# A graph-attention layer and a ternary FFN on one core: the first layernorm spread over three engines, ten inspection pieces moved to the output projection, k2 three pairs ahead

## The chip, the cores and the metric

One NeuronCore of a Trainium2 chip runs the whole program. The time is the device time of one execution in microseconds (us); of several executions the median is given. The profile comes from one further execution, taken by the hardware profiler.

## The reference

All tensors are float32. x has 384 rows (nodes) of 1024. There are 12288 edges with a source, a destination and a type.

```python
def layernorm(x): return (x - mean(x)) / sqrt(var(x) + 1e-5)          # along the row

def gnn(x):                                          # 16 heads of 64
    q, k, v = x @ wq.T + bq, x @ wk.T + bk, x @ wv.T + bv             # 1024 -> 1024 each
    q2, k2, v2 = q @ wiq.T + biq, k @ wik.T + bik, v @ wiv.T + biv    # again, then split into heads
    w = softplus(edge_type_weights)
    mask = full((384, 384), -inf); mask[src, dst] = w[type - 1]       # the last edge of a cell wins
    diagonal: where it is -inf, w[3]
    scores = q2 @ k2.T / 8 + mask                    # per head
    return (softmax(scores) @ v2) @ wo.T + bo

def ffn(x):                                          # weights in {-1, 0, 1}
    h = silu((x @ w1.T) * w1_s) * ((x @ w2.T) * w2_s)                 # 1024 -> 512
    h = gelu((h @ h1.T) * h1_s)                                       # 512 -> 512
    h = gelu((h @ h2.T) * h2_s)                                       # 512 -> 512
    return (h @ w3.T) * w3_s                                          # 512 -> 1024

x = x + gnn(layernorm(x))
x = x + ffn(layernorm(x))
```

## The kernel before

The 384 rows are three row tiles of 128 (`NT`), the 1024 features eight blocks of 128 (`KF`). A projection that keeps its result transposed (`matmul_T`, line 141: features on the partitions, 384 rows along the free dimension) adds eight products per output block; one that keeps rows on the partitions (`matmul_R`, line 150) adds eight products of 512 columns. A float32 product is two TensorE instructions in the profile.

Tile, the layer in which the kernel is written, sets all semaphores. Line 57 fixes the order on SyncE, ScalarE, VectorE and TensorE to that of the source: each of these engines runs its instructions in the order in which they are written, and one that waits holds up all behind it on its engine. This holds for the DMAs that SyncE and ScalarE issue too. POOL's order is Tile's own. A buffer of a pool comes free for the next tile with its tag when the last reader of the old one is done.

**Front.** ScalarE's queue loads the four edge type weights (`wt`), the edges (`ed`, three rows per partition) and the per-feature vectors (`vec`); SyncE's queue loads the three tiles of x (line 65) and the first half of wq. POOL makes the identity, a diagonal mask and two small tables (lines 189 to 197). VectorE computes the start of softplus, two constants (`later`, `bare`) and the edge keys source*384 + destination (lines 201 to 213), and then, tile by tile, statistics, mean and deviation, scales and the left half of the normalised row (`layernorm`, line 120); ScalarE computes the square root and the right half. `transpose_in` (line 132) turns each tile on TensorE, and ScalarE copies it into `xT`.

**Mask.** The keys are written to memory and read back as rows, eight columns at a time (`keys`, line 247). `targets` (line 256) sends an edge that is followed by another of the same cell to a spare cell. `scatter` (line 276) writes 128 edge values at once into a table in memory by an indirect DMA from POOL; each of the 96 waits for the one two before it. At the end the table is read back as `nmask` (line 300), which attention adds to its scores. Line 291 writes the table's start (`bare`), and lines 292 and 298 prefetch weights in between.

**Projections.** q, q2, v, v2 and k follow in this order, 64 products each (48 wider ones for v2). Weights come in halves of 2 MB through a pool of four buffers: after each half `prefetch` queues the next load, which waits for the oldest buffer.

**Inspection.** The FFN weights are ternary in the inputs at hand. The kernel checks this: `inspect` (line 310) loads 16 pieces of 128 x 1024 of w1, w2, h1, h2 and w3 and ORs their bits into `bits`, two VectorE instructions a piece. Four pieces follow q in the source, six follow q2, six v2. After k the 512 columns are halved down to one, summed over the partitions on TensorE and kept as `flag` (lines 352 to 362). If no low bit is set, `rest(True)` computes the FFN with rounded weights and a two-part split of the activations; otherwise `rest(False)` computes it in full float32. Line 471, ahead of the output projection, loads the flag into a register of every engine, on which the branch of line 610 depends.

**Attention.** A unit is one pair of heads and one row tile, 24 in all. Each turn of the loop of line 449 writes the scores of unit u, the transposes of unit u-2, every third turn the weighted sum of a pair, and some of the 64 products of k2: 16 (two blocks, that is two pairs of heads) stand ahead of the loop, 48 are spread over the first 20 turns.

**Output projection.** For each row tile two halves of wo are applied (`project_out`, line 490): eight products, then VectorE adds the result to x and takes statistics. `layernorm` follows, and `transpose_x2` turns the tile for the FFN: tile 0 after tile 1 is projected, tile 1 between the halves of tile 2, tile 2 within the FFN. PSUM holds three such results (`ps_mm`).

## Time and profile before

| | us |
|---|---|
| three runs | 434.35, 2401.24, 434.09; median 434.35 |
| profiled execution | 432.71 |
| its span, first to last instruction | 430.8 |
| TensorE busy | 407.4 |
| VectorE busy | 177.4 |
| POOL busy | 111.8 |
| ScalarE busy | 100.1 |
| first product of q | 18.8 |
| first and last scatter | 25.1, 228.2 |
| mask used first | 238.9 |
| first product with wo | 330.6 |
| first product of the FFN | 373.3 |

In a line of the timeline or of a group stand the engine (PE is TensorE, PEld its weight loads, DVE VectorE, ACT ScalarE, SPq the DMAs that SyncE issues), the line of the source, the operation, output and input by their names, and in brackets how long the engine was idle before and what ended that. In the chain of waits each line is a piece of the path that ended last: start, length and what it was. The slices divide the span into 40 equal parts; a digit is the busy share in tenths.

### The profile page before, as it was taken

The page shows a single profiled execution, that of the slowest core. Times are in us where ns is not written, and L with a number is a line of the kernel's source. Part 1 is how long each engine was busy: PE and PEld are TensorE (multiplying, and loading weights), DVE is VectorE, ACT ScalarE, POOL GpSimd, SP SyncE. Part 2 cuts the span into 40 slices and gives each one's busy share as a digit, 9 for nine tenths or more (in the row PEclk, how much of TensorE's full clock was granted, in tenths as well). Part 3 has the DMA queues.
Part 4 walks back from the last instruction along what each step waited for, and adds up shares of the span by engine and source line. Part 5 has one row for each costly group of instructions (what it writes and reads, how often), then busy time and mean ns, then how long its engine had stood idle before and what let it go on. Part 6 is the DMA issues. An engine that isn't in the chain of part 4 may idle for free.

```text
span 430.8 us, 4238 instructions
## 1 busy us (share of the span) xinstructions
PE 407.4 (95%) x1515; PEld 239.7 (56%) x1515; DVE 177.4 (41%) x562; ACT 100.1 (23%) x221; POOL 111.8 (26%) x117
## 2 busy tenths in 40 slices
PE   0799999999999999999999899999999999999992
PEld 0555555555555544455555455555545444699982
DVE  2945869422240011005400476655663133423354
ACT  4511111111111000001111555445464011131420
POOL 3023335243344574754374400000000000200000
PEclk9999999999999999999999999999999999999998
DMA  7699766979764405066706104100060000750012
GB/s 253 219 359 245 257 164 161 390 265 339 273 175 168 174 21 196 0 234 205 247 0 209 41 2 136 60 1 0 2 195 2 0 0 0 212 179 2 1 50 100
DMA packets 28023, 59.64 MB, mean 138 GB/s; under 512 B 4352, under 2 KB 5216, under 8 KB 27872
## 3 DMA queue, kind: packets, MB, share of 16 engines
q1 hardware_dynamic: 20688, 50.12, 34.8%
q0 software_dynamic: 6880, 9.03, 7.4%
q8 instruction: 14, 0.23, 0.2%
q10 hardware_dynamic: 432, 0.18, 0.1%
q14 instruction: 9, 0.07, 0.0%
HBM read 57.06 MB, written 2.26 MB: 138 GB/s over the span
## 4 chain that ended last, share of the span: by engine, by line
PE 77%; DMA 11%; DVE 5%; POOL 2%; issue 2%; ACT 2%; ACTq 0%; DVEq 0%; POOLq 0%
PE ps L146 29%; PE ps L155 19%; PE ps L379 7%; PE ps L516 6%; PE sc L395 4%; PE pp L428 4%; PE av L437 4%; DMA tab<-val,cell 4%; PE ps L529 3%; POOL tab L278 2%; DMA raw<-in_h 2%; DMA ed<-in_edges 2%; DMA out<-y 2%; DMA nmask<-tab 1%; DVE st L102 1%
## 5 line engine op out<-in xcount | busy, mean ns | idle before, releaser
L278 POOL DMA_INDIRECT tab<-val,cell x96 | 96.5, 1005 | 128.6 <-DMA tab<-val,cell 75.1
L262 DVE SCALAR_TENSOR_TENSOR jk<-kr,key,later 128x256 bf16<-128x256 f32 x96 | 39.9, 479 | 14.8 <-DMA kr<-keyd 14.8
L379 PE MATMUL ps<-kT,wik 128*128 128x384 f32 x128 | 45.6, 493 | 0.0
L146 PE MATMUL ps<-xT,wq 128*128 128x384 f32 x128 | 43.0, 500 | 0.0
L317 DVE TENSOR_TENSOR bits<-bits,raw 128x512 int32<-128x512 int32 x32 | 22.1, 692 | 50.7 <-DMA raw<-in_w 39.0
L155 PE MATMUL ps<-wo,aT 128*128 128x512 f32 x96 | 41.8, 593 | 0.0
L146 PE MATMUL ps<-qT,wiq 128*128 128x384 f32 x128 | 41.4, 486 | 0.0
L146 PE MATMUL ps<-xT,wv 128*128 128x384 f32 x128 | 41.4, 486 | 0.0
L146 PE MATMUL ps<-xT,wk 128*128 128x384 f32 x128 | 41.4, 486 | 0.0
L155 PE MATMUL ps<-wiv,vT 128*128 128x512 f32 x96 | 41.4, 592 | 0.0
L409 DVE CUSTOM_DVE_ANT_0 s<-sc,nmask 128x384 f32<-128x384 f32 x48 | 24.8, 553 | 26.0 <-PE sc L395 14.2
L146 PEld LDWEIGHTS ps<-xT,wq 128*128 128x128 f32 x128 | 25.0, 196 | 17.6 <-issue 1.2
L146 PEld LDWEIGHTS ps<-xT,wk 128*128 128x128 f32 x128 | 24.3, 190 | 17.2 <-issue 0.5
L146 PEld LDWEIGHTS ps<-qT,wiq 128*128 128x128 f32 x128 | 24.3, 190 | 17.0
L146 PEld LDWEIGHTS ps<-xT,wv 128*128 128x128 f32 x128 | 24.3, 190 | 17.0
L379 PEld LDWEIGHTS ps<-kT,wik 128*128 128x128 f32 x128 | 22.6, 190 | 15.5 <-issue 4.1
L155 PEld LDWEIGHTS ps<-wiv,vT 128*128 128x128 f32 x96 | 18.2, 190 | 22.7 <-issue 22.5
L155 PEld LDWEIGHTS ps<-wo,aT 128*128 128x128 f32 x96 | 18.0, 190 | 22.1 <-issue 22.1
L412 ACT ACTIVATE e<-s,lo 128x384 f32<-128x384 f32 x48 | 29.1, 609 | 3.2 <-DVE lo L409 3.1
L516 PE MATMUL ps<-x,w 128*128 128x384 f32 (+2 forms) x176 | 25.8, 306 | 0.0
L395 PE MATMUL sc<-k2T,q2T 64*128 64x384 f32 x96 | 23.5, 535 | 2.1 <-DVE lo L409 2.1
L344 DVE TENSOR_TENSOR v<-ps,row 128x512 f32<-128x512 f32 x6 | 4.2, 692 | 51.8 <-PE ps L155 51.8
(100 smaller groups left out, 355.2 us busy)
## 6 DMA issues: line engine op xcount, KB each, us to landing
kr<-keyd SPq DMA_DIRECT2D x11, 576.0 KB, 5.8
raw<-in_w SPq DMA_DIRECT2D x12, 512.0 KB, 4.8
w<-in_w POOLq DMA_DIRECT2D x3, 2048.0 KB, 9.5
wq<-in_wq SPq DMA_DIRECT2D x2, 2048.0 KB, 11.0
wiq<-in_wiq SPq DMA_DIRECT2D x2, 2048.0 KB, 14.1
wv<-in_wv SPq DMA_DIRECT2D x2, 2048.0 KB, 16.5
wiv<-in_wiv SPq DMA_DIRECT2D x2, 2048.0 KB, 10.0
wk<-in_wk SPq DMA_DIRECT2D x2, 2048.0 KB, 8.3
```

The costliest lines, as they stand in the source:

```text
L146: nc.tensor.matmul(ps[:, :N], lhsT=w[:, k, o * P:(o + 1) * P], rhs=src[:, k, :], start=(k == 0), stop=(k == nk - 1))
L155: nc.tensor.matmul(ps[:, :w.shape[2]], lhsT=src[:, k, t * P:(t + 1) * P], rhs=w[:, k, :], start=(k == 0), stop=(k == nk - 1))
L262: nc.vector.scalar_tensor_tensor(jk[:, :w], krf[:, j * P:j * P + w], key[:, c:c + 1], later[:, :w], op0=ALU.is_equal, op1=ALU.mult, accum_ ...
L278: i = nc.gpsimd.indirect_dma_start(out=tab, in_=val[:, c:c + 1], in_offset=None, out_offset=bass.IndirectOffsetOnAxis(ap=cell[:, c:c + 1], ...
L317: nc.vector.tensor_tensor(bits, bits, raw[:, h * FH:(h + 1) * FH].bitcast(I32), op=ALU.bitwise_or)
L379: nc.tensor.matmul(ps[:, :N], lhsT=wik[o // 4][:, k, o % 4 * P:(o % 4 + 1) * P], rhs=kT[:, k, :], start=(k == 0), stop=(k == KF - 1))
L395: nc.tensor.matmul(sc[:, :N], lhsT=q2T[r, pair, t * P:(t + 1) * P], rhs=k2T[r, pair, :], start=True, stop=True)
L409: nc.vector.tensor_tensor_reduce(s, sc[:, :N], nmask[:, t, :], 1.0, 3e38, op0=ALU.add, op1=ALU.min, accum_out=lo)
L412: nc.scalar.activation(e, s, AF.Exp, bias=lo, scale=-1.0, accum_out=dens[u][:, j:j + 1])
L428: nc.tensor.transpose(pt[:, m, :], e[:, m * P:(m + 1) * P], ident)
L437: nc.tensor.matmul(av[j * D:(j + 1) * D, :N], lhsT=v2[:, m, h * D:(h + 1) * D], rhs=pTs[pair % 2][:, j * NT + m, :], start=(m == 0), stop= ...
L516: nc.tensor.matmul(ps[:, rows], lhsT=w[:, k, o * P:(o + 1) * P], rhs=x[:, k, rows], start=n == 0, stop=n == len(todo) - 1)
```

## The change

The front is written out. x comes first: the left half of tile 0 on SyncE's queue and its right half on ScalarE's, then tiles 1 and 2 on SyncE's, and the edges behind the half on ScalarE's. `vec` and `wt` are loaded between two parts of the first half of wq. `later` and `bare` are made on POOL. The steps of the three tiles are interleaved; POOL computes the left half of tiles 0 and 1, VectorE that of tile 2, and copies out of PSUM are shared by ScalarE and VectorE. TensorE transposes the identity 24 times at the start and four times after tile 0. The keys are computed before tile 2 is scaled and written after the last copy; softplus follows.

```diff
-    wt = const.tile([P, 4], FP, name="wt")
-    nc.scalar.dma_start(wt, bass.AP(tensor=etw.tensor, offset=etw.offset, ap=[[0, P], [1, 4]]))
+    xs = act.tile([P, NT, F], FP, name="xs")
+    for queue, c in ((nc.sync, slice(0, FH)), (nc.scalar, slice(FH, F))):
+        queue.dma_start(xs[:, 0, c], x[:P, c])
+    for t in (1, 2):
+        nc.sync.dma_start(xs[:, t, :], x[t * P:(t + 1) * P, :])
     ed = const.tile([P, 3, NCOL], I32, name="ed")
     nc.scalar.dma_start(ed, edges)
-    xs = act.tile([P, NT, F], FP, name="xs")
-    for t in range(NT):
-        nc.sync.dma_start(xs[:, t, :], x[t * P:(t + 1) * P, :])
-    nc.scalar.dma_start(vec, vecs)
+    def load_small():
+        nc.sync.dma_start(vec, vecs)
+        nc.sync.dma_start(wt, ...)
...
-    prefetch()
+    prefetch(load_small)                 # wq's first half in two parts, load_small between
...
+        nc.gpsimd.tensor_scalar(later, jp, 0.0, None, op0=ALU.is_gt)
+        nc.gpsimd.tensor_scalar(bare, nmask, 0.0, FAR, op0=ALU.is_equal, op1=ALU.mult)
...
+        with tc.tile_pool(name="ps_up", bufs=5, space=bass.MemoryType.PSUM) as ps_up:
+            warm(24)
+            statistics(0, sts[0], 0)
+            statistics(0, sts[0], 1)
+            deviation(0)
+            statistics(1, sts[1], 0)
+            scales(0)
+            normal(0, nc.gpsimd)
+            turned(0)
+            warm(4)
+            statistics(1, sts[1], 1)
+            deviation(1)
+            evicted(0, 0, nc.scalar.copy)
+            statistics(2, sts[2], 0)
+            scales(1)
+            normal(1, nc.gpsimd)
+            turned(1)
+            statistics(2, sts[2], 1)
+            deviation(2)
+            evicted(0, 1, nc.scalar.copy)
+            nc.vector.tensor_copy(edf, ed[:, 0:2, :])
+            nc.vector.scalar_tensor_tensor(key, edf[:, 0, :], float(N), edf[:, 1, :],
+                                           op0=ALU.mult, op1=ALU.add)
+            scales(2)
+            normal(2, nc.vector)
+            kt = ps_mm.tile([P, 512], FP, tag="mm", name="kt")
+            nc.tensor.transpose(kt[:NCOL, :P], key, ident)
+            turned(2)
+            evicted(1, 0, nc.vector.tensor_copy)
+            evicted(1, 1, nc.scalar.copy)
+            evicted(2, 0, nc.vector.tensor_copy)
+            evicted(2, 1, nc.scalar.copy)
+            nc.vector.tensor_copy(keyr, kt[:NCOL, :P])
+            nc.sync.dma_start(keyd, keyr)
```

The helpers do what their names say: `warm(n)` transposes the identity n times, `deviation` is the mean, variance and square root, `scales` the reciprocal and the scaled mean, `normal(t, engine)` the left half on that engine and the right half on ScalarE, `turned` the eight transposes, `evicted` one of the two copies out of PSUM.

The inspections after q and q2 go; the six after v2 stay. The other ten, the halving and the flag move into the output projection. Three of them at a time use a buffer of the tag "t" (that of qT, vT, kT and pTa).

```diff
         qT = project(xT, "qT", vec[:, BQ:])
-        inspect(4)
         project(qT, "q2T", biqs, dst=q2T, scale=-0.125)
-        inspect(6)
...
-    low_bits = nc.values_load(flag[0:1, 0:1], min_val=0, max_val=P * 0xFFF)
...
+    inspect_more(True, 2)                # three pieces in a buffer "t", two in "stage"
     for t in range(NT):
         st = small.tile([P, 2, 6], FP, name="st")
         project_out(t, 0, st)
-        if t == 2:
+        if t == 0:
+            inspect_more(True)
+        elif t == 1:
+            bitf = gather_bits()
+        else:
             transpose_x2(1)
         project_out(t, 1, st)
         layernorm(t, xn[:, t, :], st)
-        if t == 1:
+        if t == 0:
+            inspect_more(False, len(pieces))
+        elif t == 1:
+            fl = ps_mm.tile([P, 512], FP, tag="mm", name="fl")
+            nc.tensor.matmul(fl[:1, :1], lhsT=bitf, rhs=ones, start=True, stop=True)
+            flag = const.tile([1, 1], I32, name="flag")
+            nc.vector.tensor_copy(flag, fl[:1, :1])
+            low_bits = nc.values_load(flag[0:1, 0:1], min_val=0, max_val=P * 0xFFF)
             transpose_x2(0)
```

Ahead of attention three blocks of k2 are computed instead of two, and the loop spreads the remaining 40 products over its first 20 turns.

```diff
+AHEAD = 3
...
-        done = 0
-        for _ in range(2 * KF):
+        done, rest_k2 = 0, (KF - AHEAD) * KF
+        for _ in range(AHEAD * KF):
             next(k2)
...
-            share = min((u + 1) * 6 * KF // (units - 4), 6 * KF)
+            share = min((u + 1) * rest_k2 // (units - 4), rest_k2)
```

## The prediction

> **What bounds the kernel now.** I read the page's busy table and its slices first, then the chain of waits in order of time, then the timeline of the places that the diff touches.

> ```profile
> PE 407.4 (95%) x1515; PEld 239.7 (56%) x1515; DVE 177.4 (41%) x562; ACT 100.1 (23%) x221; POOL 111.8 (26%) x117
> PE   0799999999999999999999899999999999999992
> ```

> TensorE is busy for 407 of 430.8 us. Its work stays the same in the change, so only what it waits for can move the time: most of the 23 us it is idle lies in the first two slices and in the last, with small holes near 240 and 320 us.

> ```profile
> 1.17 7.04 DMA ed<-in_edges
> ...
> 18.92 125.42 PE ps L146 x384
> ...
> 228.18 5.53 DMA tab<-val,cell
> ...
> 234.33 4.31 DMA nmask<-tab
> ...
> 330.69 27.66 PE ps L155 x64
> ```

> This is the chain: the edge list holds up the layernorm, then TensorE runs unbroken, then the mask read back from the table opens attention (first use 238.87), then TensorE again. Between the ends stands a second chain that TensorE doesn't see until 238: 96 scatters on POOL, one after another.

> ```profile
> 8.23 0.26 DVE L210 CAST edf<-ed 128x192 f32<-128x192 int32 x1 [0.84 <-DMA ed<-in_edges]
> ...
> 18.77 11.41 PE L146 MATMUL ps<-xT,wq 128*128 128x384 f32 x30
> ...
> 20.21 0.34 PEld L146 LDWEIGHTS ps<-xT,wq 128*128 128x128 f32 x1 [0.30 <-issue]
> ...
> 20.85 0.34 PEld L146 LDWEIGHTS ps<-xT,wq 128*128 128x128 f32 x1 [0.30 <-issue]
> ...
> 91.68 0.96 POOL L278 DMA_INDIRECT tab<-val,cell  x1 [3.68 <-DMA tab<-val,cell]
> ...
> 226.90 0.97 POOL L278 DMA_INDIRECT tab<-val,cell  x1 [0.30 <-issue]
> ```

> VectorE can't start on x (landed at 0.75+5.4 = 6.2 us) before the edges are in, and the first projection starts at 18.8. Its first instructions come 0.64 us apart, later ones 125.42/384 = 0.327. Each matmul of the source is two such instructions (64 per projection, x128 in the page), so one costs 0.653 us. The scatters are 1.27 us apart where nothing else moves and wait 3 to 5 us more per pair under bulk loads.

> ```profile
> 358.19 1.04 PE L485 MATMUL pt<-ident,xn 128*128 128x128 f32 x8
> ...
> 358.39 0.69 DVE L493 TENSOR_TENSOR xs<-ps,xs 128x512 f32<-128x512 f32 x1 [5.38 <-PE ps L155]
> ...
> 360.69 0.54 DVE L123 TENSOR_SCALAR xn<-xs,mv,rs 128x512 f32<-128x512 f32 x1
> ```

> At the end of row tile 1 in the wo stage TensorE goes straight on, while VectorE still has 2.9 us of layernorm before it.

> [...] 0.64 against 0.327 us, though TensorE was 70% busy from 11.5 to 17 us; only the unbroken run from 17 released it, near 21.5. [...] scatters land 2.1 us (median) after issue in 127 to 186 us, where the DMA share is 0.33, and 5.3 in 75 to 127, where it is 0.82. [...]

> **Part 1, front.** The chain after, with rows of before. x tile 0 goes over two queues ahead of the edges' 384 small rows: I take it landed at 5.0 instead of 6.2, tile 1 at 7.5 instead of 7.9, tile 2 near 9. In VectorE's order the first half statistics of tile 1 (0.68) stand before the scales of tile 0 (0.16+0.16): so tile 0 can be normalised from 8.6. GpSimd's half isn't in the trace; [...] the tensor add of line 349 is 2.32 for 1024 with two inputs. I take 1.0 (0.8 to 1.5). The two constants moved to POOL (1152 and 256 elements, 1.5 to 3.2 us from the same rows) follow its last iota at 4.1 and end by 7.3, hidden by the wait for x. From 8.6 ScalarE is longest: three half rows (0.81), two square roots (0.30), four copies (0.59) are 5.4 us, plus 0.4 of waiting for GpSimd and the first transposes: 14.4. VectorE's last copy, which the first four products need, ends near 14.2. Projection starts at 14.3: **4.5 us** gained (3.3 to 5.5). wq's first half needs x, edges and 1 MB, 2.65 MB; before, that much had moved by 10.5 us, so it is in.

> 24 transposes of the identity at 0.24 us (1.94 for eight) run from 2.3 to about 8 without a hole, so the clock is probably up[...]. Before, the first 30 instructions took 11.41 instead of 30 x 0.327 = 9.8: **1.6 us** gained (0 to 1.6).

> **Part 2, scatter chain.** The keys now leave after the evictions: 13.9 + 3.3 landing + 3.6 for the first row block = 20.8, against 18.6. Exp and Ln with two table loads (1.28 each) go from 14.4 to 17.4 on ScalarE, before the first projection's copy; negw is there at 17.5. The second half of wq is queued on SP behind keys and `bare` as before, near 19 + 9.4, needed at 14.3 + 21 = 35. First scatter 27.2 instead of 25.06: 2.1 us later. Against that ten inspection loads (5 MB) leave the time of the scatters. From 25 to 229 the chain took 204 us where 96 x 1.27 = 122 would do: 82 us over, for 24 MB of weights (second half of wq to first half of wo), 6.8 of key rows, 8.4 of inspections and 1.6 of bias rows, 41 MB: 2.0 us per MB. Ten pieces are 5.2 MB, so 10.4 us (7 to 15). The mask then lands at 238.65 + 2.1 - 10.4 = 230.4. TensorE comes to attention at 237.4 - 6.1 + 5.2 (eight matmuls of k2 more, 8 x 0.653) = 236.5. The mask is no longer late.

> **Part 3, third pair ahead.** k2's work is moved, not removed: nothing by itself. Within attention the filler falls from 2.4 to 2 matmuls per unit; a unit without the weighted sum is then 0.84 + 0.81 + 1.31 = 2.96 us, and units of that length already run without a stall (274.86 to 277.81). With the mask in time the hole of 1.25 us at 242.4 shrinks to the pipeline's fill: **0.7 gained** (0.2 to 1.25).

> **Part 4, inspection in wo.** Ten pieces x 2 x 0.69 = 13.8 us and the halvings (2.5 with the two small ones) go to VectorE. Five pieces (7.0) fit between its last copy (328.5) and the first eviction (337.9). Three (4.2) fit before the second, two (2.8) into the 4.1 us idle before the third, the halvings into the 5.4 before the fourth. Their loads are on SP, which has nothing else then; the first trio waits for kT (free near 314, sharing the DMAs with w2), the second for pTa (free at 326), 1.5 MB each, some 6 us. No eviction is late by this.

> The flag now becomes ready inside the wo stage, and `values_load` puts a wait for it and a register load on every engine, TensorE too, in program order ahead of the transposes of tile 0. VectorE copies the flag only after tile 1's layernorm: from the page, 361.23 + about 0.2 = 361.4. TensorE, ready at 358.19, waits 3.2 us. The load itself isn't in the trace: at its old place (330.6) it is hidden. [...] **3.8 us lost** (3.3 to 4.5), and queued behind it are the rest of wo and the FFN, all TensorE work. [...]

> **Sum.** -4.5 - 1.6 - 0.7 + 3.8 = -3.0. The profiled execution took 432.71 (span 430.8): 429.7. The median of the three runs, 434.35, is 1.6 above it: **431.3**; its own range is 429.5 to 432.8 by the bounds above.

> **Rivals.** (a) The flag doesn't stop TensorE, because its load isn't in its stream ahead of the transposes or matmuls are queued past it: 434.35 - 6.8 = 427.5. For it: before, no gap at the load. Against: there the flag was 100 us old. (b) Slower: the mask takes the bound. If taking the inspections away doesn't speed up the scatters (other loads only move into their place, the table's own write time rules), the mask lands 2.1 late, at 240.8. The front's gain is then idle ahead of attention, which is 5.2 shorter: 2.1 - 5.2 + 3.8 = +0.7, **435.0**. It begins to bind when the scatters win under 4.3 us, and makes the kernel slower under 0.7. For it: scatters of 30 to 60 us are slow with no inspection near. Against: 36 scatters in 59 us at a share of 0.33, 20 in 52 at 0.82. (c) The front gains little: x lands no sooner than before, GpSimd takes 1.5 us a half, or the clock drops in the gaps between transposes: start at 15.8 and no clock gain, -3.0 - 0.7 + 3.8, 434.4.

> **Chances.** Forecast 0.5, (a) 0.17, (b) 0.13, (c) 0.2. The range goes from (a) to near (c): 427.4 to 434.8. A change over 2% (8.7 us, about what a measurement here can tell from none) needs two rivals at once either way: faster 0.05, same 0.91, slower 0.04.

> **What would show it.** First projection near 14.3 with instructions 0.33 apart; first scatter near 27, last near 222; the mask in before the first scores; a TensorE gap of 3 to 4 us in wo ahead of the transposes of tile 0, with the flag copy before its end. I am wrong if that gap is missing, if TensorE idles for the mask, or if wo's evictions wait for inspections.

## The result and the profile after

The changed kernel takes 435.25 us in the median (433.13 to 436.41), the kernel before, measured on the same chip, 434.22. The ratio is 1.002, with a 95% interval of 1.000 to 1.004: about a microsecond slower, within what counts as no change here. (Ratios are of executions at the usual speed; the one of 2401 us before the change isn't among them, and what made it long is not known.) The forecast, 431.3, was too low by 4. The profiled execution took 436.12 (span 434.3), against 432.71 (430.8) before.

Cut at the same events as the forecast's sum, the two profiled executions differ as follows (us; the last column is the stretch after minus before):

| stretch | before | after | difference |
|---|---|---|---|
| start to first product of q | 18.77 | 17.69 | -1.1 |
| first product of q to first product with wo | 311.85 | 308.94 | -2.9 |
| first product with wo to first product of the FFN | 42.65 | 48.05 | +5.4 |
| first product of the FFN to first multiply of the output | 42.08 | 42.07 | 0 |
| from there to the end | 15.45 | 17.55 | +2.1 |

The last row doesn't follow the change: in the profiles of the kernels below, none of which edits that stretch, it is 15.3 in two that have most of the change (e2 and e7), 17.6 in one that has little of it (b1) and 16.7 to 17.5 in the rest. A wait for an output write holds the last columns in the long ones (2.4 to 3.3 us, against 0.8 in the profile of before). Without it the profiles differ by +1.4, the medians by +1.0.

First the busy table and the slices of the changed kernel:

```profile
PE 412.0 (95%) x1543; PEld 245.4 (57%) x1543; DVE 179.0 (41%) x560; ACT 99.8 (23%) x219; POOL 118.3 (27%) x121
...
PE   4999999999999999999999999999999969999990
...
PEclk9799999999999999999999999999999998999997
```

TensorE is busy for 4.6 us more, but not with more work of the layer: the 28 transposes of the identity alone take 5.9 us, which is why the first slice is fuller. New is the 6 in slice 33 (347 to 358 us), which was full before: the wo stage. The granted clock has a dip right behind it (the 8 in slice 34), faint in slices of 10.9 us each, and a deeper one in the front (the 7 in slice 2).

The chain of waits of the changed kernel, in order of time:

```profile
4.18 4.13 POOL bare L215
9.25 2.09 POOL xn L244
11.38 1.97 PE pt L256 x8
13.35 0.85 PE pw L227 x4
14.21 1.71 PE pt L256 x8
...
17.69 124.11 PE ps L143 x384
...
224.28 15.49 PE ps L426 x48
...
357.88 1.81 PE pt L531 x8
359.70 7.80 PE ps L152 x16
```

Two things have changed from before. The front hangs on POOL until 11.34, where it hung on the edge list, and then on TensorE's transposes at half speed, four of the identity (`pw`) among them; and the mask, which stood in the chain at 234.33, is gone: TensorE goes from k to k2 to the scores. What is left of the hole in the first unit is 0.40 us, where it was 1.25.

The timeline of the changed kernel at the front:

```profile
4.18 4.12 POOL L215 TENSOR_SCALAR bare<-nmask 128x1152 f32<-128x1152 f32 x1
...
6.42 0.14 DVE L237 RECIPROCAL rs<-sd 128x1 f32<-128x1 f32 x1
6.60 1.37 DVE L239 SCALAR_TENSOR_TENSOR mr<-mv,rs 128x1 f32<-128x1 f32 x1
...
8.38 0.87 POOL L213 TENSOR_SCALAR later<-jp 128x256 f32<-128x256 int32 x1
9.25 4.14 POOL L244 TENSOR_SCALAR xn<-xs,mv,rs 128x512 f32<-128x512 f32 x2
...
17.69 2.52 PE L143 MATMUL ps<-xT,wq 128*128 128x384 f32 x7 [0.35 <-DVE xT L259]
```

The scale that POOL's half of tile 0 needs is ready at 6.56 (6.42 + 0.14). POOL is busy with the two constants until 9.25, and then needs 2.07 us for each half row. On VectorE the same half row takes 0.54. TensorE, whose first 24 transposes end at 7.15, has nothing to do for 4.2 us. Stretches of 3.41 us show what that does to its clock (the third number from the end):

```profile
6.46:9.87 3.41, 0.69 (x6) 0.46 (x4) 3.31 (x8) 1.11 (x2) 3.33 (x3) 1.00 1.00 332
9.87:13.29 3.42, 1.91 (x9) 1.91 (x10) 2.25 (x5) 0.76 (x2) 3.42 (x2) 0.50 0.82 275
13.29:16.70 3.41, 3.41 (x18) 3.40 (x17) 1.49 (x4) 2.60 (x5) 0.10 (x1) 0.50 0.11 33
```

From 9.87 to 16.70 TensorE runs at half clock: what the 24 transposes had gained is lost. POOL's second half row ends at 13.39, before TensorE is through with what stands ahead (14.21).

The same view of the wo stage, where row tile 1 ends:

```profile
354.29 0.19 PE L575 MATMUL fl<-ones,bitf 128*1 128x1 f32 x2
...
357.16 0.14 DVE L577 CAST flag<-fl 1x1 int32<-1x1 f32 x1
...
357.88 1.81 PE L531 MATMUL pt<-ident,xn 128*128 128x128 f32 x8 [3.40 <-DVE flag L577]
...
360.35 0.34 PEld L152 LDWEIGHTS ps<-wo,aT 128*128 128x128 f32 x1 [0.52 <-issue]
...
361.75 0.19 PEld L152 LDWEIGHTS ps<-wo,aT 128*128 128x128 f32 x1 [0.24 <-issue]
```

TensorE stands still for 3.40 us until the flag is in its register, 0.58 after VectorE's copy ended (357.30 to 357.88). Then the eight transposes take 1.81 where they take 1.04 to 1.06 warm, and weight loads of 0.34 with 0.52 between them show half clock until about 361.4; from 361.75 they are 0.19 again. Stretches of 2 us of the changed kernel, with busy times of the engines and, third from the end, the granted clock, show it directly:

```profile
core 0: us, PE busy (x) PEld busy (x) DVE busy (x) ACT busy (x) POOL busy (x), PEclk, DMA share, GB/s
...
356.00:358.00 2.00, 0.12 (x1) 0.15 (x2) 0.90 (x5) 1.11 (x2) 0.00 (x0) 1.00 0.00 0
358.00:360.00 2.00, 2.00 (x9) 1.83 (x9) 0.45 (x1) 0.85 (x2) 0.00 (x0) 0.51 0.00 0
360.00:362.00 2.00, 2.00 (x4) 0.84 (x3) 0.94 (x2) 0.32 (x1) 0.00 (x0) 0.64 0.00 0
362.00:364.00 2.00, 2.00 (x6) 0.86 (x5) 0.00 (x0) 0.00 (x0) 0.00 (x0) 1.00 0.00 0
```

The 5.4 us of the wo stage are so 3.7 of wait (3.4 of pause; 0.3 stay in e1 below, which has no pause) and 1.7 of half clock.

### The profile page after: what moved, and what is told of

Same layout as the page of the kernel before. It is cut to its first block, busy times and chain, and to the rows that moved or that the text cites. A ratio compares the mean times of both kernels' runs of the same rounds, so it can differ in the third digit from the quotient of the medians.

```text
span 434.3 us, 4296 instructions
## 1 busy us (share of the span) xinstructions
PE 412.0 (95%) x1543; PEld 245.4 (57%) x1543; DVE 179.0 (41%) x560; ACT 99.8 (23%) x219; POOL 118.3 (27%) x121
## 4 chain that ended last, share of the span: by engine, by line
PE 90%; DVE 3%; POOL 2%; DMA 2%; ACT 2%; issue 1%; ACTq 0%; POOLq 0%; DVEq 0%
PE ps L143 38%; PE ps L152 19%; PE ps L426 9%; PE ps L591 6%; PE sc L442 4%; PE pp L475 4%; PE av L484 4%; PE ps L604 3%; DMA out<-y 2%; PE pt L256 1%; POOL bare L215 1%; PE pt L531 1%; ACT e L459 1%; DVE y L681 1%; DVE y L682 1%
## 5 line engine op out<-in xcount | busy, mean ns | idle before, releaser
L353 POOL DMA_INDIRECT tab<-val,cell x96 | 93.7, 976 | 111.6 <-DMA tab<-val,cell 69.3
L456 DVE CUSTOM_DVE_ANT_0 s<-sc,nmask 128x384 f32<-128x384 f32 x48 | 24.7, 552 | 44.9 <-PE sc L442 44.9
L152 PE MATMUL ps<-wo,aT 128*128 128x512 f32 x96 | 42.8, 604 | 0.0
L143 PE MATMUL ps<-xT,wq 128*128 128x384 f32 x128 | 41.5, 487 | 0.3 <-DVE xT L259 0.3
L182 DVE TENSOR_TENSOR bits<-bits,raw 128x512 int32<-128x512 int32 x32 | 22.1, 691 | 14.6 <-DMA raw<-in_w 13.8
L92 POOL DMA_DIRECT2D w<-in_w x3 | 2.6, 870 | 84.8 <-PE ps L426 80.8
```

The source lines that it names most:

```text
L143: nc.tensor.matmul(ps[:, :N], lhsT=w[:, k, o * P:(o + 1) * P], rhs=src[:, k, :], start=(k == 0), stop=(k == nk - 1))
L152: nc.tensor.matmul(ps[:, :w.shape[2]], lhsT=src[:, k, t * P:(t + 1) * P], rhs=w[:, k, :], start=(k == 0), stop=(k == nk - 1))
L182: nc.vector.tensor_tensor(bits, bits, raw[:, h * FH:(h + 1) * FH].bitcast(I32), op=ALU.bitwise_or)
L353: i = nc.gpsimd.indirect_dma_start(out=tab, in_=val[:, c:c + 1], in_offset=None, out_offset=bass.IndirectOffsetOnAxis(ap=cell[:, c:c + 1], ...
L456: nc.vector.tensor_tensor_reduce(s, sc[:, :N], nmask[:, t, :], 1.0, 3e38, op0=ALU.add, op1=ALU.min, accum_out=lo)
```

## The experiments

The theory after the result: (1) the front gave little because of what was put on POOL, and (2) the moved flag costs a stop of TensorE and a stretch at half clock behind it. The rivals: the front is held by the order of its steps or by x; the loss in wo comes from inspections that make evictions late; the inspections had to move for the mask; the third pair or the warm-up do something of their own.

All ratios are to the kernel before on the same chip, with 95% intervals. "q" is the first product of q, "wo" the wo stage as in the table above, both from the profiled execution.

| kernel | q | wo | mask read back, first use | median | ratio |
|---|---|---|---|---|---|
| before | 18.77 | 42.65 | 234.3, 238.9 | | 1 |
| changed | 17.69 | 48.05 | 220.5, 240.6 | 435.25 | 1.002 (1.000 to 1.004) |
| e1_flag_late | 17.76 | 42.92 | 225.4, 240.7 | 430.47 | 0.9907 (0.9872 to 0.9942) |
| e6_flag_before_ln | 17.11 | 46.64 | 224.5, 240.1 | 432.42 | 0.9975 (0.9956 to 0.9995) |
| e2_consts_dve | 14.29 | 49.19 | 220.4, 237.2 | 430.85 | 0.9917 (0.9887 to 0.9947) |
| e3_norm_dve | 13.01 | 49.04 | 220.1, 236.0 | 430.71 | 0.9912 (0.9877 to 0.9946) |
| e4_ahead2 | 16.75 | 49.31 | 220.1, 234.5 | 435.20 | 1.0047 (1.0030 to 1.0064) |
| e5_inspect_old | 17.67 | 42.65 | 232.6, 240.9 | 430.20 | 0.9921 (0.9894 to 0.9947) |
| e7_norm_cold | 12.92 | 49.20 | 217.6, 235.9 | 431.85 | 0.9956 (0.9936 to 0.9976) |
| e8_best | 12.99 | 42.93 | 216.7, 235.9 | 425.42 | 0.9811 (0.9780 to 0.9841) |
| e9_best_old | 13.18 | 42.65 | 229.6, 236.4 | 425.93 | 0.9806 (0.9760 to 0.9852) |
| e10_fill | 16.63 | 46.37 | 220.0, 239.6 | 432.88 | 0.9987 (0.9968 to 1.0006) |
| b1_ahead3 | 18.59 | 42.65 | 225.9, 244.0 | 433.18 | 0.9981 (0.9960 to 1.0002) |
| b2_inspect_moved | 18.75 | 46.37 | 218.1, 237.4 | 436.63 | 1.0069 (1.0029 to 1.0108) |

The kernel before took 434.22 beside the changed kernel, 434.38 beside e1, e2, e3 and e6, 432.99 beside e4, e5, e7 and e8, and 433.46 beside the rest. Medians of different groups are therefore compared by their ratios.

### The front: constants, half rows, warm-up

**e2_consts_dve**

```diff
-        nc.gpsimd.tensor_scalar(later, jp, 0.0, None, op0=ALU.is_gt)
-        nc.gpsimd.tensor_scalar(bare, nmask, 0.0, FAR, op0=ALU.is_equal, op1=ALU.mult)
...
             nc.sync.dma_start(keyd, keyr)
+        nc.vector.tensor_scalar(later, ...)
+        nc.vector.tensor_scalar(bare, ...)
```

> The changed kernel with the two constants of the front made on VectorE behind the key copy instead of on POOL ahead of the normalisation. Theory (POOL, 5.0 us busy with the constants, starts the first half row 2.5 us late, and is slow at the half rows too): first half row on POOL from 6.8 instead of 9.25 us and still about 2 us long, first projection from about 15 instead of 17.7, time about 432.6. Rival (POOL isn't what sets the front; ScalarE's chain or x is): start above 17, time above 434.5.

In the timeline POOL takes the half rows as soon as the scales are there, and the first product comes at 14.29:

```profile
6.99 4.15 POOL L242 TENSOR_SCALAR xn<-xs,mv,rs 128x512 f32<-128x512 f32 x2 [2.90 <-DVE rs L235]
...
9.13 1.97 PE L254 MATMUL pt<-ident,xn 128*128 128x128 f32 x8 [2.56 <-POOL xn L242]
...
14.29 3.17 PE L143 MATMUL ps<-xT,wq 128*128 128x384 f32 x9 [0.35 <-DVE xT L257]
```

3.4 us earlier, by the two constants alone; on VectorE they cost 0.28 and 0.75 and stand behind the keys, where nobody waits for them.

**e3_norm_dve**

```diff
 e2_consts_dve, and
-            normal(0, nc.gpsimd)
+            normal(0, nc.vector)
-            normal(1, nc.gpsimd)
+            normal(1, nc.vector)
```

> As the run with the constants on VectorE, and the left halves of tiles 0 and 1 normalised on VectorE too (0.54 us each in the profile of before), so that POOL has no part in the layernorm. Theory (POOL's price of about 2 us for half a row is the rest of the loss): first projection from about 14.0 us, the instructions 0.33 apart from the start since TensorE's gaps are short, time about 431.6; VectorE's small instructions, which took up to 1.4 us beside POOL, take 0.2. Rival (VectorE becomes the bound of the front): start at 15 or later, no better than with POOL.

```profile
6.82 0.54 DVE L242 TENSOR_SCALAR xn<-xs,mv,rs 128x512 f32<-128x512 f32 x1
...
13.01 3.17 PE L143 MATMUL ps<-xT,wq 128*128 128x384 f32 x9 [0.34 <-DVE xT L257]
13.07 0.28 DVE L293 TENSOR_SCALAR later<-jp 128x256 f32<-128x256 int32 x1
13.27 0.75 DVE L294 TENSOR_SCALAR bare<-nmask 128x1152 f32<-128x1152 f32 x1
```

Another 1.28 us earlier. So POOL's share of the front costs 4.7 us of start in all, the clock that fell behind it included: in e3 TensorE's gaps are short (0.49 us at most from 7.50 to q) and the clock stays up, in e2 it is at half from 8.68 to 12.09. The written-out order without POOL would have brought 5.8. The medians of e2 and e3 can't be told apart (their intervals overlap); that e3 starts earlier rests on the timeline. With the changed kernel's own front the start lies between 16.6 and 17.8 in the table. POOL lets TensorE go at 11.38 or 11.39 in all six of these profiles; the rest is the clock, which comes up at 14.52 in e10 and 14.77 in e4 (start at 16.63 and 16.75), at 15.51 in e6 (17.11), and at 16.7 to 16.8 in the three that start at 17.67 to 17.76.

**e7_norm_cold**

```diff
 e3_norm_dve, and
-            warm(24)
-            warm(4)
```

> The run with constants and half rows on VectorE, without the 28 transposes of the identity. Theory (they raise the clock early and the short gaps keep it up): the transposes of the three tiles take 0.24 us each instead of 0.13, the first projection starts about 1 us later (14.0) and its first instructions are 0.64 us apart[...]: 2 to 2.5 us more than with them, about 433. Rival (the clock is up by the first projection anyway): within 0.7 of the run with them, about 431.

The start (12.92 us against 13.01) and the stretch from the first product of q to wo (309.50 against 309.51) are the same: in these two profiles the warm-up does nothing. The transposes of tiles 0 and 1 run at 0.25 us each, those of tile 2 at full speed (1.09 us for eight), so the clock is up before q either way; at half speed TensorE has hardly a pause between the tiles (16 transposes from 7.42 to 11.4, the next eight from 11.48). But each is one execution, and when the clock comes up differs from one to another. By the ratio e7 is 0.4% above e3, on another chip and with intervals that just overlap, so a gain from the warm-up on average isn't excluded.

### The flag: where the wait stands, and what the pause does to the clock

**e1_flag_late**

```diff
         elif t == 1:
             ...
-            low_bits = nc.values_load(flag[0:1, 0:1], ...)
             transpose_x2(0)
+    low_bits = nc.values_load(flag[0:1, 0:1], ...)       # behind the loop over t
```

> The changed kernel with one line moved: the load of the flag into the engines' registers stands after the last row tile of the output projection instead of after tile 1. Theory (the wait for the flag costs 3.5 us of TensorE's time and the clock drop behind it 1.9): the wo stage falls from 48.5 to 43.1 us as before the change, the time from 435.25 to about 429.9, ratio to before 0.990. Rival (the wo stage is long because of the ten inspections on VectorE, and the wait only shows where they end): the stage stays above 46 us and the time above 433.

The wo stage falls from 48.05 to 42.92, no wait and no half clock. The ten inspections are still in it, at a cost of at most 0.3 us (42.65 before). Moving that one line is worth 1.1% of the time.

**e6_flag_before_ln**

```diff
+        if t == 1:
+            (product for the flag, and its copy)
         layernorm(t, xn[:, t, :], st)
         ...
         elif t == 1:
-            (product for the flag, and its copy)
             low_bits = nc.values_load(flag[0:1, 0:1], ...)
```

> The changed kernel with the flag's sum and copy ahead of the layernorm of tile 1, its load where it was. The wait gets shorter but stays: VectorE has the add and the statistics before the copy (1.5 us), then 0.1 for the copy and 0.6 for the load, so TensorE waits 2.2 instead of 3.5 us. Theory (the half-speed stretch after the wait is the clock[...]): the eight transposes behind it take 0.9 us instead of 1.8 and the sixteen products 6.9 instead of 7.8, so 1.3 + 1.9 = 3.2 us are won, about 432. Rival (the stretch is slow for another reason, such as refilling the queue or PSUM, at any wait): only 1.3 us are won, about 434.

The wait shrinks as expected, to 1.97 us, and the transposes behind it run at full speed (1.06 us). But wo is 46.64, not 44.9 (48.05 - 3.2): the half clock comes all the same, later. The timeline, and then stretches of 3.41 us of the same kernel, laid so that one ends where the half clock begins:

```profile
353.72 0.19 PE L572 MATMUL fl<-ones,bitf 128*1 128x1 f32 x2
355.88 1.06 PE L531 MATMUL pt<-ident,xn 128*128 128x128 f32 x8 [1.97 <-DVE mv L122]
```

```profile
353.43:356.84 3.41, 1.44 (x12) 1.08 (x12) 2.41 (x7) 0.83 (x2) 0.00 (x0) 1.00 0.00 0
356.84:360.25 3.41, 3.41 (x6) 1.35 (x6) 1.29 (x2) 1.24 (x3) 0.00 (x0) 0.50 0.00 0
360.25:363.66 3.41, 3.41 (x10) 1.50 (x9) 0.00 (x0) 0.00 (x0) 0.00 (x0) 1.00 0.00 0
```

A stretch in which TensorE was busy for 1.44 of 3.41 us is followed by one at half clock. My expectation, which had all that stands behind a wait of 2.2 us at full speed, was wrong.

**e10_fill**

```diff
             flag = ... ; nc.vector.tensor_copy(flag, fl[:1, :1])
+            pw = ps_ff.tile([P, 4, P], FP, tag="ff", name="pw")
+            for i in range(26):
+                nc.tensor.transpose(pw[:, i % 4, :], ident, ident)
             low_bits = nc.values_load(flag[0:1, 0:1], ...)
```

> Changed kernel with 26 transposes of the identity put on TensorE between the product for the flag and the load of the flag, so that TensorE works (26 x 0.109 = 2.8 us) while VectorE finishes tile 1's layernorm. Theory (the slow stretch after the wait is the half clock that the idle 3.4 us brought on): the flag is waited for as before, but the eight transposes and the products behind the load run at full speed, wo shrinks from 48.05 to about 46.1 us, time about 1.9 below the changed kernel's 435.25: 433.3. Rival (the slow stretch comes from the load, or from weights or results that are late): wo stays at 48, time stays.

```profile
353.37 3.06 PE L580 MATMUL pw<-ident 128*128 128x128 f32 x26
356.83 1.07 PE L531 MATMUL pt<-ident,xn 128*128 128x128 f32 x8 [0.41 <-issue]
```

TensorE still resumes 3.4 us after the flag's product, since it must wait for the flag; only it isn't idle. The transposes take 1.07, wo is 46.37: 1.7 less than in the changed kernel, as the theory had it. So the slow stretch comes from the pause, not from the load or from what follows it; that this isn't the luck of one execution rests on the timed executions, below. The ratio falls from 1.002 to 0.9987; the intervals just overlap.

**b2_inspect_moved**: the kernel before with the inspection's move alone (first layernorm and the two pairs ahead as before).

```diff
-        inspect(4)                       # after q
-        inspect(6)                       # after q2
...                                       # halvings, product, flag and its load likewise
+    inspect_more(True, 2)                # in wo, as in the changed kernel
```

> Kernel before with the inspection's move alone. Theory: scatters end 10 to 15 us sooner, the mask is early and the hole ahead of attention shrinks by 0.85; the wo stage waits 3.5 for the flag and pays 1.9 to 3 at half clock behind it: 434.2 - 0.85 + 5.4 to 6.5 = 438.8 to 439.9. Rival (in this place the clock holds, as the forecast had it): 434.2 - 0.85 + 3.8 = 437.2.

```profile
356.81 0.19 PE L515 MATMUL fl<-ones,bitf 128*1 128x1 f32 x2
360.40 1.06 PE L471 MATMUL pt<-ident,xn 128*128 128x128 f32 x8 [3.40 <-DVE flag L517]
```

The move by itself costs 0.7% (3.0 us). The same wait of 3.40 us here is not followed by half clock: the transposes take 1.06, wo 46.37. The rival's ratio (437.2 to 434.2, 1.007) is the measured one; the theory's, 1.011 to 1.013, lies at the upper end of the interval or beyond it.

Why both? The half clock comes in pieces of one length. Behind the pause it lasts 3.41 us in the changed kernel and in e6, 6.83 in e2, e3, e4 and e7, and doesn't come in b2 and e10. The wo stage is accordingly 46.37, 48.05, or 49.0 to 49.3 us with none, one or two pieces behind the same wait. The pause need not be as long as a piece: in e6 one of 1.97 us was enough.

Every trace shows where its windows lie: each stretch between two changes of the clock is a whole multiple of 3.413 us (3.41, 6.83, 68.27 and 341.33 in the changed kernel: 1, 2, 20 and 100), so in these traces the clock changes only at their ends. In the changed kernel it comes up at 16.70 and falls at 358.03, 100 windows apart. In b2 it falls after the last product, at 430.16; 21 windows before that is 358.48. First e2 on its windows, then b2 on its own:

```profile
350.02:353.43 3.41, 1.08 (x5) 0.21 (x3) 1.95 (x6) 0.30 (x1) 0.00 (x0) 1.00 0.00 0
353.43:356.84 3.41, 2.34 (x9) 2.10 (x10) 1.03 (x3) 1.77 (x3) 0.00 (x0) 0.50 0.00 0
356.84:360.25 3.41, 3.41 (x5) 1.35 (x4) 0.84 (x2) 0.22 (x1) 0.00 (x0) 0.50 0.00 0
360.25:363.66 3.41, 3.41 (x9) 1.52 (x8) 0.00 (x0) 0.00 (x0) 0.00 (x0) 1.00 0.00 0
```

```profile
355.07:358.48 3.41, 1.93 (x7) 0.59 (x5) 1.50 (x3) 0.00 (x0) 0.00 (x0) 1.00 0.00 0
358.48:361.89 3.41, 1.49 (x10) 1.28 (x11) 1.09 (x6) 1.88 (x4) 0.00 (x0) 1.00 0.00 0
...
426.75:430.16 3.41, 0.00 (x0) 0.00 (x0) 0.85 (x2) 0.00 (x0) 0.00 (x0) 1.00 0.34 117
430.16:433.57 3.41, 0.00 (x0) 0.00 (x0) 0.85 (x2) 0.00 (x0) 0.00 (x0) 0.50 0.12 42
```

In e2 a window busy for 1.08 us lowers the clock, the next, busy for 2.34, doesn't raise it, and a full one does. In b2 the pause is split over two windows, busy for 1.93 and 1.49, and neither lowers it. All 14 traces, laid on their windows (1752 in all), agree without exception: at full clock each window in which TensorE was busy for 1.44 us or less (e6) was followed by half clock, and none busy for 1.49 or more (b2) was; at half clock each busy for 2.68 or less (14.93 to 18.34 in the kernel before) was followed by another at half, and each busy for 2.95 or more (8.68 to 12.09 in e2) by full clock. (The record of the clock begins with its first rise; what lies ahead of it counts as half, as the 0.24 us of a transpose there show.) Where a pause falls on the windows decides between none, one and two pieces.

The timed executions bear it out. Each has its mean granted clock; (1 - clock) x span is the time's worth of clock that it lost, over the whole span, idle time in the front and at the end included. Its mean is 7.4 us in the changed kernel and 7.3 in e6, against 5.9 in e1 and 5.8 in e10, which have the same front and no idle pause: 1.4 to 1.6 us for the pause. With the old front it is 3.2 in b2 (eight executions, from 1.3 to 6.6) against 2.4 in b1: 0.8, no more than the scatter of such a mean. With the front of e3 it is 4.8 in e3 against 2.4 in e8, on another chip: 2.4. So on average the pause costs about 0.8 to 2.4 us of clock. In the profiles it cost the wo stage between 0 and 2.9 us of time (46.37 to 49.31).

### The third pair

**e4_ahead2**

```diff
-AHEAD = 3
+AHEAD = 2
```

> The changed kernel with two pairs of k2 ahead of attention, as before the change. Theory (the mask has landed by 225 us, long before the first scores, so the third pair only moves work of TensorE): first scores at about 234.5 instead of 239.7, attention 5.2 us longer, the time from the first projection to the output projection unchanged at 309 us within 0.4, time 435.25 within 1. Rival (the third pair fills holes of attention): that stretch 1 to 2 us longer, time above 436.5.

The scores start 6.1 earlier (0.9 of it from an earlier start), and the stretch from q to wo is the same to 0.01 us (308.94). With the mask in early the third pair does nothing in the profile. The ratios, 1.0047 and 1.002, have intervals that overlap; the equal medians, 435.20 and 435.25, are from groups in which the kernel before differs by 1.2 us and show nothing.

**b1_ahead3**: the kernel before with three pairs ahead.

```diff
-        for _ in range(2 * KF):
+        for _ in range(3 * KF):
             next(k2)
...
-            share = min((u + 1) * 6 * KF // (units - 4), 6 * KF)
+            share = min((u + 1) * 5 * KF // (units - 4), 5 * KF)
```

> Kernel before with the third pair of k2 alone. The mask lands at 238.65 as before, the first scores move from 237.4 to 242.6, and the hole of 1.25 us in the first unit shrinks to 0.4 (the changed kernel's): 0.85 off, 433.4. Rival (the hole is the fill of the pipeline and not the mask, or is given back in longer units later): no change, 434.2.

The hole shrinks only from 1.25 to 0.96, with the mask read back 18 us ahead of its first use, so most of the hole in that kernel is the fill of the pipeline and not the mask. b2, with the mask early too, has the same 0.96. The remaining 0.56 to the 0.40 of the changed kernel is ScalarE's load of the table for the exponential (1.28 us), which starts 0.07 us after the mask's first use in the seven kernels in which POOL normalises half rows, and 0.63 after it in the other seven; why is open. The stretch from q to wo is 311.95 (311.85 before), and the interval of the ratio reaches over 1. The scatters took 198.3 us here and 203.1 in the profile of before, with the same loads around them: so much they differ from one execution to another.

### Did the inspections have to move?

**e5_inspect_old**: the changed kernel with the ten pieces, the halvings, the flag and its load where they were before the change.

```diff
+        inspect(4 pieces)                # after q, as before
+        inspect(6 pieces)                # after q2, as before
...                                       # halvings, product and flag after k; load ahead of wo
-    inspect_more(True, 2)                # and what follows from it in wo
```

> The changed kernel with all 16 inspections and the flag at their places of before; the new front and the third pair stay. The wait for the flag is gone (5.4 us won in wo). Theory (each piece that loads among the scatters costs them 1.5 us: they took 203 us before and 188 after): the scatters take about 203 us from 29.6, the mask lands near 242, TensorE is at the first scores at 239.8 and waits 2 to 3 us and then runs up to 3.4 us at half clock: 432 to 435. Rival (the inspections don't hold up the scatters): mask by 230, time 429.9.

The rival's time (429.9) is met, but not for its reason: the scatters do slow down, from 188.1 to 196.9 us. The mask is read back at 232.6, and with the 4.3 us that it took to land in the kernel before it is there at 236.9; it is first used at 240.9. It is 4 us early.

**e9_best_old**: e3_norm_dve and e5_inspect_old together.

```diff
 later, bare, normal(0), normal(1): nc.gpsimd -> nc.vector, the constants behind the keys
 inspection, halvings, flag and its load: as before the change
```

> Constants and half rows of the front on VectorE, and the inspection, its sum and the flag's load where they were before the change; third pair kept. Theory (the move of the ten pieces is not needed once attention starts later relative to the mask): scatters take about 197 us, the mask is read back by 232 against a first use at 236, no wait for it, wo 42.7: 425.5, as with the flag loaded behind the loop. Rival (the front's 5 us bring attention ahead of the mask): the mask comes some us late and the time is 427 to 430.

In the timeline the mask is read back and used:

```profile
229.57 0.80 POOL L376 DMA_DIRECT2D nmask<-tab  x1 [1.79 <-DMA tab<-val,cell]
...
236.44 0.56 DVE L469 CUSTOM_DVE_ANT_0 s<-sc,nmask 128x384 f32<-128x384 f32 x1 [16.37 <-PE sc L455]
```

229.57 + 4.3 is 233.9, 2.6 us before its first use; the wait there is for the scores. 425.93: not moving the inspections at all is as good as moving them and loading the flag late. The margin is less than the 5.2 us by which the third pair puts off the scores, so here the third pair probably has a use; that was not tried.

### Both losses taken away

**e8_best**: e3_norm_dve and e1_flag_late together.

```diff
 later, bare, normal(0), normal(1): nc.gpsimd -> nc.vector, the constants behind the keys
 values_load: behind the loop over t
```

> Both repairs together: constants and half rows of the front on VectorE, and the load of the flag behind the last row tile. Theory (the two losses are separate): first projection at 13, wo stage 43.1, so 4.7 + 5.4 us less than the changed kernel: about 425.5, ratio to before 0.980. Rival (a front that is earlier is lost again at the mask or in wo): above 428.

The ratio is 0.9811, where 0.980 was expected: 1.9% (1.6 to 2.2) below the kernel before. The two losses are separate and add up: 13.0 for the start, 42.93 for wo.

## Why the prediction was wrong

By its own sum, each term against the profiles:

| term | forecast | measured |
|---|---|---|
| front, start of q | -4.5 | -1.1 |
| clock in q | -1.6 | -1.5 |
| hole ahead of attention | -0.7 | -0.85 |
| wait for the flag | +3.8 | +3.7 |
| half clock behind that wait | 0 | +1.7 |
| small pieces from q to wo | 0 | -0.6 |
| sum | -3.0 | +1.4 |

**Two terms failed.** The first is in Part 1, the price of GpSimd. The 1.0 us for a half row, with bounds of 0.8 to 1.5, was my estimate, and the one row that the trace had (2.32 us in the forecast, 2.36 in the profile, for 1024 elements with two inputs) seemed to bear it out. It took 2.07. For the two constants I had 1.5 to 3.2 us and named the wait for x as their cover; they took 4.12 and 0.87, and the cover was shorter than assumed: tile 0's statistics started at 4.08 and POOL's scale was ready at 6.56, not 8.6. Together they keep POOL in the chain from 4.18 to 11.34 and TensorE idle from 7.15 to 11.38. In that pause the clock falls (half from 9.87 to 16.70), where Part 1 had it "probably up", and the transposes behind it run at half speed, with 0.85 us for the four of the identity, which did no good there. Of 4.5 us 1.1 was left. With the constants off POOL the start is 14.29, the 14.3 that was forecast, but that is luck: POOL's scale is ready 1.7 us earlier than assumed (6.89 in e2), and each half row takes 1.07 longer.

The second is in Part 4. Its sum has nothing for the clock behind the wait; that the clock holds there was my estimate, and no trace had shown it. Six of the seven profiles with an idle pause there have it, with one or two pieces; in e6 a window in which TensorE works for 1.44 of 3.41 us was idle enough. On average over the timed executions it costs 0.8 to 2.4 us.

The forecast's own range doesn't follow from its bounds either: the best of each term add up to -5.05 and the worst to +1.0, which is 429.3 to 435.4 for the median, not 429.5 to 432.8. The measured 435.25 would lie inside, but by way of a clock that gains nothing in q, and it did gain.

**What held.** The wait for the flag was found from the order of VectorE's instructions and is 3.40 us of pause (3.8 forecast, 3.2 of it from that order; the rest, for the register load, was an estimate without a trace), with 0.58 from the flag's copy to TensorE's next transpose. The ten inspections fit between the evictions (e1). The mask is no longer late, by more than was forecast: the scatters took 188.1 us where 203.1 minus 10.4 was 192.7, and start at 29.6, not 27.2, because the front ends late. In b2, with the old front, the move alone shortened them to 190.3, by 8 to 13 us (against 198.3 in b1 and 203.1 in before), where 10.4 was forecast. Over all profiles they take 188.1 to 193.1 in the ten with the pieces moved and 196.9 to 203.1 in the four without, 9.6 apart in the mean. The third pair is worth nothing by itself in the profiles. The hole came out near its size, but only 0.3 us of it is the mask (b1, b2). The clock term did too (q ran at half clock from 18.77 to 21.76 before, and never after), but not by its reason: the clock that the 24 transposes had raised was lost again, and the window from 13.29 to 16.70, full of transposes at half speed, raised it just ahead of q.

**The rivals.** Rival (c) described the place: GpSimd slow, and the clock lost in a gap. Its start was 15.8, the measured 17.7; it gave up the clock's gain in q, which came. Its time, 434.4, is near the result, and (b)'s, 435.0, is nearer still by chance, with a mechanism that didn't occur. Rival (a) is refuted by the pause, and (b) by the mask, read back 20 us before its first use.

## What to carry to other kernels

Before work goes to a spare engine, look for what that engine does at the moment the result is wanted, and price the operation by the worst row at hand: a constant that seemed free stood ahead of the one instruction for which TensorE waited. The load of a register stands in program order on the engine that loads it, and here it was a wait of 3.40 us for TensorE; put it behind the last instruction that doesn't depend on it (e1: 42.92 us in wo for 48.05). A pause of 2 to 3.4 us of TensorE must be priced with what it does to the clock, up to another 2.9 us here, and where it can't be removed, work thrown away in it can keep the clock up (e10: 1.07 us for the transposes behind it, where they took 1.81).
